# The last image's 3x3 convolution computed by pairs of rows

## The chip, the cores and the metric

The kernel runs on one core of a Trainium2 chip. The metric is the device time of one execution in microseconds (us), as a median of several runs. Engines are named as in the profile: PE is TensorE (matmul), PEld its weight load, DVE is VectorE, ACT is ScalarE, POOL is GpSimd, and SP is SyncE, whose queue issues the transfers (DMA).

## What is computed

The input `x` holds 4 images of 128 channels and 64x64 pixels, all float32. Four layers follow one another, each of the form "x plus a block applied to the group-normalised x": an attention over the 4096 pixels, a 5x5 convolution with built weights, a state-space scan in two directions, and a plain 3x3 convolution. The change touches the last layer alone, and of that only the last image:

```python
def conv2d(x, w, b, stride=1, pad=1):
    y = jax.lax.conv_general_dilated(x, w, window_strides=(stride, stride), padding=[(pad, pad), (pad, pad)], ...)
    return y + b[None, :, None, None]
...
out = conv2d(x, main_w, main_b, stride=1, pad=1)      # 128 channels to 128, 3x3
...
# --- layer 3 (conv_preact) ---
x = x + _L3_conv_ref(_gn(x), ...)
```

(The offset branch of that layer chooses between `out` and `out`, so it isn't computed.)

## The kernel before

Channels lie on the 128 partitions and pixels on the free axis. An image has 4096 pixels, cut into 4 chunks of `CH` = 1024 pixels (16 rows) or 8 pieces of `MM` = 512 (8 rows, one PSUM bank of float32).

The order of the instructions on each engine is written by hand. `scan_core` is the backbone: it emits the ticks of the state-space scan of images 0 to 3 one after the other, and between the half ticks it lets a generator, `images`, emit pieces of all the other work (attention and the 5x5 convolution of later images, the end of earlier ones). A tick puts one product on GpSimd (`drive`, L1027), a decay on ScalarE (L1020), a recurrence on VectorE (L1037), a second product on VectorE or GpSimd (L1040 or L1058), and a sum over states on TensorE (L1072). For images 0 to 2 the last layer (`back`, which calls `conv`) lies beside the scan of later images. For image 3 there is no later image: when the last tick is done, the loop `for _ in chain(end(B - 1, range(PER)), back(B - 1))` emits the rest, and the program ends with it.

The last image's layer in that tail works so. `end` adds the scan's result to the residual `xt` (L1134, L1135, L1137) and collects sums for the group norm. `conv` clears the borders of a padded image `xpm`, calls `group_norm` (a row of small VectorE and GpSimd instructions, ending in `rs_m` L363 and `nb_m` L364), and normalises `xt` into `xpm` on ScalarE in four pieces of 16 rows (L369). Then it runs over the 8 pieces of 512 pixels. For each, 9 products (a 128x128 weight by 128x512 pixels) are summed into one bank `pcm` (L643). A piece's result goes to `finish`, here `put`: one VectorE instruction adds the bank, the bias `MAINB` and the residual `xt` (L1222), and a transfer of 256 KB writes the piece out (L1223).

The 3x3 weights `m3` are the first nine 128x128 matrices of the tile `cw`. That tile holds the 5x5 weights until the last image's 5x5 convolution (`conv_pairs`, L760) is over; a transfer then loads `main_w` over its head, in `front`. `kept` is a copy of those nine matrices of the 5x5 weights in memory, taken at the start for a second pass (`program(True)`), which runs only where a sum of the attention left its range; the test for it (`pfit`, `out_of_range`, L1338 to L1340) are the program's last instructions.

PSUM has eight banks. The tail has one each under the tags `s`, `a`, `z` and `y`, and four in the pool `wide`, in which the scan's decays `da` lie, two tiles of two banks. The pool `hc` holds six tiles of 128x1024 for the scan's products.

Of the kernel before, what the change touches and what calls it, by code (L numbers as in the profile page):

```python
# [24 lines left out]
F32 = mybir.dt.float32  # L25
I32 = mybir.dt.int32
AF = mybir.ActivationFunctionType
ALU = mybir.AluOpType
# [4 lines left out]
P = 128  # L33
GROUPS = 32
GN_EPS = 1e-5
CH = 1024
MM = 512
# [8 lines left out]
PRODUCT, HOP, SLOT, PACE, ENDPACE, AHEAD = 0.86, 1.7, 0.7, 2.8, 1.5, 4  # L46


BQ, BK, BX, BP, CONVB, BD, DSKIP, MAINB, CONVW, ALOG = 0, 1, 2, 3, 4, 5, 6, 7, 8, 12
# [3 lines left out]
def conv_preact_kernel(  # L53
# [16 lines left out]
    nc = tc.nc  # L70
    B, C, H, W = x.shape
    L = H * W
    NCH = L // CH
# [11 lines left out]
    of = out.rearrange("b c h w -> b c (h w)")  # L85
# [3 lines left out]
    dram = ctx.enter_context(tc.tile_pool(name="dram", bufs=2, space=DRAM))  # L89
    ps = ctx.enter_context(tc.tile_pool(name="ps", bufs=1, space=PSUM))  # L90
    pools, ready = {}, set()

    def bank(tag, name):
        return pools.get(tag, ps).tile([P, MM], F32, tag=tag, name=name)
# [32 lines left out]
    def col(i):  # L127
        return vec[:, i : i + 1]
# [93 lines left out]
    cw = const.tile([P, NTAP + 10, C], F32, name="cw")  # L222
    taps5 = cw[:, :NTAP, :]

    m3 = cw[:, : main_w.shape[1], :]
    kept = dram.tile([P, main_w.shape[1], C], F32, tag="kept", bufs=1, name="kept")

    def build_conv_weights(tmp):
        xx_sb = tmp.tile([P, NTAP, C], F32, name="xx_sb")
        nc.sync.dma_start(xx_sb, xhat)  # L230
        id_sb = tmp.tile([P, C], F32, name="id_sb")
        nc.sync.dma_start(id_sb, identity)
        picked = tmp.tile([P, 2, NTAP, C // 2], F32, name="picked")
        for n, (which, table, inds) in enumerate((("xx", wxx, indsxx), ("id", wid, indsid))):
            nr, oc = table.shape[1], table.shape[2]
            acc = picked[:, n]
            one = cw.rearrange("p k c -> p (k c)")[:, : NTAP * oc]
            one = one.rearrange("p (k o) -> p k o", o=oc)
            tab = tmp.tile([P, nr, oc], F32, name=f"tab{which}")
            nc.sync.dma_start(tab, table)  # L240
            ii = tmp.tile([P, NTAP], I32, name=f"ii{which}")
            nc.sync.dma_start(ii, inds.to_broadcast([P, NTAP]))
            fi = tmp.tile([P, NTAP], F32, name=f"fi{which}")
            nc.vector.tensor_copy(fi, ii)

            ng = tmp.tile([P, NTAP], F32, name=f"ng{which}")
            nc.vector.tensor_scalar(ng, fi, 0.0, float(nr), ALU.is_lt, ALU.mult)
            nc.vector.tensor_tensor(fi, fi, ng, ALU.add)
            nc.vector.tensor_scalar(fi, fi, 0.0, float(nr - 1), ALU.max, ALU.min)
            for r in range(nr):  # L250
                hit = tmp.tile([P, NTAP], F32, name=f"hit{which}{r}")
                nc.vector.tensor_scalar(hit, fi, float(r), None, ALU.is_equal)
                hit_b = hit.unsqueeze(2).to_broadcast([P, NTAP, oc])
                tab_b = tab[:, r : r + 1, :].to_broadcast([P, NTAP, oc])
                if r == 0:
                    nc.vector.tensor_tensor(acc, tab_b, hit_b, ALU.mult)
                else:
                    nc.vector.tensor_tensor(one, tab_b, hit_b, ALU.mult)
                    nc.vector.tensor_tensor(acc, acc, one, ALU.add)
                yield HOP  # L260

        for t in range(2):
            def every(ap):
                return ap.rearrange("p k (o t) -> p k o t", t=2)[:, :NTAP, :, t]

            idb = id_sb.rearrange("p (o t) -> p o t", t=2)[:, :, t].unsqueeze(1)
            idb = idb.to_broadcast([P, NTAP, C // 2])
            nc.vector.tensor_tensor(every(xx_sb), every(xx_sb), picked[:, 0], ALU.mult)
            nc.vector.tensor_tensor(every(cw), picked[:, 1], idb, ALU.mult)
            yield HOP  # L270
        nc.vector.tensor_tensor(taps5, taps5, xx_sb, ALU.add)
        for n in range(2):
            row = cw[:, (1 + 2 * n) * 5 :]
            nc.vector.tensor_tensor(
                cw[:, NTAP + n * 5 : NTAP + (n + 1) * 5, :], row[:, :5], row[:, 5:10], ALU.add
            )
        nc.sync.dma_start(kept, m3)

# [1 line left out]
    ASIZE, VSIZE = HP * (W + PAD) + PAD, (H + 2) * (W + 2) + PAD  # L282
# [85 lines left out]
    def normalise(dst, src, gn):  # L368
        nc.scalar.activation(dst, src, AF.Identity, scale=gn[0], bias=gn[1])  # L369
# [244 lines left out]
    def conv(b, xs, tag, st, weights, k, finish, name, residual=False):  # L614

        pad = k // 2
        hp, wp = H + 2 * pad, W + 2 * pad
        size = VSIZE if tag == "V" else ASIZE
        xp = pools["big"].tile([P, size], F32, tag=tag, name=f"xp{name}_{b}")
        xp = xp[:, : hp * wp].rearrange("p (h w) -> p h w", w=wp)  # L620
        nc.gpsimd.memset(xp[:, :pad, :], 0.0)
        nc.gpsimd.memset(xp[:, hp - pad :, :], 0.0)
        nc.gpsimd.memset(xp[:, pad : hp - pad, :pad], 0.0)
        nc.gpsimd.memset(xp[:, pad : hp - pad, wp - pad :], 0.0)
        gn = yield from group_norm(st, f"{name}{b}")
        xh = xs.rearrange("p (h w) -> p h w", w=W)

        def piece(i):
            h0, h1 = i * H // 4, (i + 1) * H // 4
            normalise(xp[:, pad + h0 : pad + h1, pad : pad + W], xh[:, h0:h1, :], gn)  # L630

        piece(0)
        yield HOP / 2
        piece(1)
        done = None
        for i in range(NM):
            if i < 2:
                piece(2 + i)
            acc = bank("saz"[i % 3], f"pc{name}_{b}_{i}")
            for t in range(k * k):  # L640
                dy, dx = divmod(t, k)
                y = i * RPM + dy
                nc.tensor.matmul(  # L643
                    acc.rearrange("p (r w) -> p r w", w=W), weights[:, t, :],
                    xp[:, y : y + RPM, dx : dx + W],
                    start=t == 0, stop=t == k * k - 1 and not residual,
                )
                if t == 2 and done is not None:
                    finish(*done)
                if t % 3 == 2:  # L650
                    yield 3 * PRODUCT
            if residual:
                nc.tensor.matmul(acc, ident, xs[:, bass.ts(i, MM)], start=False, stop=True)
            yield PRODUCT
            done = i, acc
        yield HOP
        finish(*done)

# [483 lines left out]
    def program(safe):  # L1144
        mats4, ynds, ends = {}, {}, {}
        ready.clear()
        if safe:
            nc.sync.dma_start(m3, kept)

        def load(tile, b):  # L1150
            for c in range(NCH):
# [15 lines left out]
        def front(b, xn, v):  # L1167

            xs = large(b + 1, f"xs_{b}")[:, :L]
            st = Sums(f"e{b}")  # L1170
            yield from attention(b, xs, xn, v, st, safe, load(xs, b))
            st2 = Sums(f"s{b}")

            yield from conv_pairs(b, xs, f"A{b % 2}", st, st2, b > 0 or safe)
            if b + 1 == B:
                nc.sync.dma_start(m3, main_w)

            def mat(name):
                return dram.tile([NCH, P, CH], F32, tag=name, name=f"{name}_{b}")

            mats4[b] = (
                [mat("bm"), mat("cm")], mat("dd"), mat("dxd"), mat("xcd"),
                dram.tile([P, L], F32, tag="xsd", bufs=B, name=f"xsd_{b}"),
            )
            ynds[b] = dram.tile([NM, P, MM], F32, tag="ynd", bufs=B, name=f"ynd_{b}")
            operands = yield from scan_prep(b, xs, st2, mats4[b])
            if b + 1 < B:
                return (yield from both(operands, start(b + 1, 10)))
            yield from operands

        def stage(b, pieces, done):

# [19 lines left out]
        def back(b):  # L1212
            xs, st, _ = ends[b]

            def put(i, acc):
                cut = bass.ts(i, MM)
                if b + 1 < B:
                    to = pools["bg"].tile([P, MM], F32, tag="w", bufs=4, name=f"o_{b}_{i}")
                    nc.scalar.activation(to, acc, AF.Identity, bias=col(MAINB))
                else:  # L1220
                    to = xs[:, cut]
                    nc.vector.scalar_tensor_tensor(to, acc, col(MAINB), to, ALU.add, ALU.add)  # L1222
                nc.sync.dma_start(of[b][:, cut], to)  # L1223

            yield from conv(b, xs, "V", st, m3, 3, put, "m", residual=b + 1 < B)

        def both(*gens):

# [173 lines left out]
```

## Time and profile before

| what | value |
|---|---|
| time, median of 3 runs | 4534.42 us (4531.9 to 4534.6) |
| span of the profiled run | 4538.3 us |
| PE busy | 4022.5 us (89%) |
| DVE busy | 3649.1 us (80%) |
| POOL busy | 3636.2 us (80%) |
| ACT busy | 2400.1 us (53%) |
| `pcm` products (L643), all four images | 576 rows, 592 ns in the median |
| `pcm` products of the last image, in the tail | 144 rows, 63.8 us |

How to read it: a product of float32 shows as two rows in the records of PE, so the last image's 72 products are 144 rows. Matmuls are pipelined, so a row's duration is more than its share of the time; the time of a run of products is read from its first start to its last end. "Idle before, releaser" is the time in which an engine had nothing to do, and what ended it. The chain of waits follows back from the last instruction to what each one waited for.

### The profile page before, as it was taken

The page shows a single profiled execution, that of the slowest core. Times are in us where ns is not written, and L with a number is a line of the kernel's source. Part 1 is how long each engine was busy: PE and PEld are TensorE (multiplying, and loading weights), DVE is VectorE, ACT ScalarE, POOL GpSimd, SP SyncE. Part 2 cuts the span into 40 slices and gives each one's busy share as a digit, 9 for nine tenths or more (in the row PEclk, how much of TensorE's full clock was granted, in tenths as well). Part 3 has the DMA queues.
Part 4 walks back from the last instruction along what each step waited for, and adds up shares of the span by engine and source line. Part 5 has one row for each costly group of instructions (what it writes and reads, how often), then busy time and mean ns, then how long its engine had stood idle before and what let it go on. Part 6 is the DMA issues. An engine that isn't in the chain of part 4 may idle for free. (4 is left out here: it accounts for less than half of the span.)

```text
span 4538.3 us, 43660 instructions
## 1 busy us (share of the span) xinstructions
PE 4022.5 (89%) x13568; PEld 1492.3 (33%) x13568; DVE 3649.1 (80%) x3619; ACT 2400.1 (53%) x4420; POOL 3636.2 (80%) x1730
## 2 busy tenths in 40 slices
PE   8999998999999979999999879999999658576767
PEld 4444433333333323333333223333333112121212
DVE  4722106999998978999989879999999699999993
ACT  3333217666665466666654566666654654544441
POOL 3433207999998969999989889999999799999992
PEclk9999999999999989999999989999999878687878
DMA  1000006445544555544545555545445566656561
GB/s 62 6 1 1 5 29 239 175 170 174 175 174 155 181 202 201 175 174 169 179 154 181 185 207 180 169 170 175 175 159 178 211 235 204 231 188 230 186 232 47
DMA packets 210579, 719.48 MB, mean 159 GB/s; under 512 B 24864, under 2 KB 25760, under 8 KB 210208
## 3 DMA queue, kind: packets, MB, share of 16 engines
q1 hardware_dynamic: 208736, 715.87, 44.8%
q8 instruction: 109, 1.79, 0.2%
q14 instruction: 134, 1.10, 0.1%
q10 hardware_dynamic: 1600, 0.73, 0.1%
HBM read 649.07 MB, written 67.44 MB: 158 GB/s over the span
## 5 line engine op out<-in xcount | busy, mean ns | idle before, releaser
L1027 POOL TENSOR_TENSOR db<-dx,br 128x1024 f32<-128x1024 f32 x1024 | 2399.7, 2366 | 234.0 <-DMA dx<-dxd 59.7
L1020 ACT ACTIVATE da<-de,a_neg 128x512 f32<-128x512 f32 (+1 forms) x1795 | 1342.2, 751 | 745.4 <-DVE da L1037 451.2
L464 PE MATMUL sc<-r,x 128*128 128x512 f32 x2048 | 1082.4, 611 | 18.2 <-ACT r L433 12.4
L476 PE MATMUL acc<-pt,v 128*128 128x512 f32 x2048 | 1046.6, 593 | 1.6
L1058 POOL TENSOR_TENSOR hc<-hc,cr 128x1024 f32<-128x1024 f32 x406 | 959.7, 2364 | 14.3 <-ACT last L1053 11.7
L470 ACT ACTIVATE pt<-sc 128x512 f32<-128x512 f32 x1024 | 604.3, 590 | 563.9 <-PE sc L464 555.2
L1072 PE MATMUL y<-hc,sel 128*32 128x512 f32 x4096 | 656.9, 651 | 271.5 <-POOL hc L1058 267.0
L1040 DVE TENSOR_TENSOR hc<-da,cr 128x512 f32<-128x512 f32 (+1 forms) x1067 | 828.4, 776 | 68.9 <-issue 1.8
L1037 DVE TENSOR_TENSOR_SCAN da<-da,last,db 128x512 f32<-128x512 f32 (+1 forms) x464 | 728.2, 1569 | 27.3 <-POOL db L1027 21.7
L1037 DVE TENSOR_TENSOR_SCAN da<-da,da,db 128x512 f32<-128x512 f32 x449 | 577.9, 1287 | 13.6 <-ACT da L1020 12.7
L464 PEld LDWEIGHTS sc<-r,x 128*128 128x128 f32 x2048 | 359.1, 190 | 605.0 <-issue 374.3
L476 PEld LDWEIGHTS acc<-pt,v 128*128 128x128 f32 x2048 | 387.5, 190 | 497.2 <-issue 477.9
L1037 DVE TENSOR_TENSOR_SCAN hc<-da,hc,db 128x512 f32<-128x512 f32 x322 | 413.1, 1283 | 61.2 <-ACT da L1020 30.4
L1037 DVE TENSOR_TENSOR_SCAN hc<-da,last,db 128x512 f32<-128x512 f32 (+1 forms) x304 | 455.9, 1500 | 6.6 <-ACT da L1020 2.4
L518 POOL TENSOR_TENSOR sidep<-sidep,pt 128x512 f32<-128x512 f32 x120 | 170.4, 1420 | 280.0 <-ACT pt L470 277.9
L1072 PEld LDWEIGHTS y<-hc,sel 128*32 128x32 f32 x4096 | 94.7, 111 | 728.5 <-POOL hc L1058 359.5
L643 PE MATMUL pcm<-xpm,cw 128*128 128x512 f32 x576 | 290.5, 652 | 30.5 <-ACT xpm L369 30.5
L760 PE MATMUL pe<-df,cw 128*128 128x512 f32 x640 | 289.5, 598 | 0.0
L518 DVE TENSOR_TENSOR sided<-sided,pt 128x512 f32<-128x512 f32 x120 | 97.2, 810 | 231.0 <-ACT pt L470 229.7
L1037 DVE TENSOR_TENSOR_SCAN da<-da,db 128x512 f32<-128x512 f32 (+1 forms) x154 | 231.2, 1501 | 32.5 <-POOL db L1027 16.4
L498 PE MATMUL zp<-pt,ones 128*32 128x512 f32 x1536 | 204.8, 595 | 5.0 <-DVE xs L562 5.0
L1053 ACT COPY last<-da 128x1 f32<-128x1 f32 x469 | 73.0, 156 | 246.9 <-DVE hc L1040 245.1
(196 smaller groups left out, 2719.5 us busy)
## 6 DMA issues: line engine op xcount, KB each, us to landing
br<-bm SPq DMA_DIRECT2D x512, 512.0 KB, 5.2
cr<-cm SPq DMA_DIRECT2D x512, 512.0 KB, 3.9
de<-dd SPq DMA_DIRECT2D x64, 512.0 KB, 4.6
dx<-dxd SPq DMA_DIRECT2D x64, 512.0 KB, 6.5
x<-in_x_dram SPq DMA_DIRECT2D x16, 512.0 KB, 5.1
xs<-in_x_dram SPq DMA_DIRECT2D x16, 512.0 KB, 5.6
xsd<-xs SPq DMA_DIRECT2D x16, 512.0 KB, 5.1
xcd<-xc SPq DMA_DIRECT2D x16, 512.0 KB, 2.8
```

The lines of the kernel that those rows point to most:

```text
L464: nc.tensor.matmul(sc, xn[:, bass.ts(j, P)], rq[blk], start=True, stop=True)
L470: nc.scalar.activation(pt, sc, AF.Exp)
L476: nc.tensor.matmul(acc[blk], v[:, j, :], ring[:, u % NRING, :], start=j == 0, stop=j == NJT - 1)
L518: eng.tensor_tensor(s, s, ring[:, u % NRING, :], ALU.add)
L643: nc.tensor.matmul(acc.rearrange("p (r w) -> p r w", w=W), weights[:, t, :], xp[:, y : y + RPM, dx : dx + W], start=t == 0, stop=t == k * ...
L760: nc.tensor.matmul(flat(acc), cw[:, w * K5 + dx, :], view(r, dx), start=k == 1, stop=k == total and (n == 0 or not lean),)
L1020: nc.scalar.activation(da, rep["de", b, c, d, g][:, bass.ts(h, size)], AF.Exp, scale=a_neg[:, at(i)])
L1027: nc.gpsimd.tensor_tensor(dbs[i], rep["dx", b, c, d, g], rows["b", b, c, d, q], ALU.mult)
L1037: nc.vector.tensor_tensor_scan(h, da, db[:, cut], before, ALU.mult, ALU.add)
L1040: nc.vector.tensor_tensor(hc[:, cut], h, rows["c", b, c, d, q][:, cut], ALU.mult)
L1058: nc.gpsimd.tensor_tensor(hcs[i], hcs[i], rows["c", b, c, d, q], ALU.mult)
L1072: nc.tensor.matmul(y[r : r + SG, :], sel, hcs[i - KG + 1 + gg][:, bass.ts(h, MM)], start=q == 0, stop=False, tile_position=(0, r), skip_gr ...
```

## The change

Two neighbouring output rows need four input rows. Call these d0 to d3, and the weights of the three rows of a 3x3 kernel g0, g1, g2 (each still with three columns). Then

- e = g0 (d0 - d2), s = (g0 + g1 + g2)/2 (d1 + d2), t = (g0 - g1 + g2)/2 (d2 - d1), o = g2 (d3 - d1)
- upper row = e + s + t, lower row = s - t + o

Four products for each of the three columns give two rows, where the direct way takes six. `conv_last` does this for image 3. Its chunk is 16 output rows, that is 8 pairs, so each of e, s, t, o is a bank of 128x512, and a chunk takes 4 banks and 12 products. It stands in for `conv` in the tail; images 0 to 2 keep `conv`.

- `last_weights` makes the two combined weights (three matrices each, `HSUM` and `HDIF`) by four VectorE instructions over 128x384, emitted when the last image's scan operands are done, early in the last image's scan. They lie in `cw` behind `m3`, so `kept` now saves and restores 15 matrices and not nine.
- `piece(c)` normalises 17, 16, 16 and 15 rows (one ahead of the chunk); the padded image has no columns at the sides, and the products of the outer columns take 63 of the 64 pixels of a row.
- `combine(c)` makes the four sums of rows: d2 - d1 and d3 - d1 on GpSimd, d1 + d2 and d0 - d2 on VectorE, into tiles of the pool `hc`.
- The banks are `s`, `a`, `z`, `y` for the even chunks and the four of `wide` for the odd ones.
- Each chunk ends with a ScalarE copy of t, two GpSimd instructions (add to the upper rows, subtract from the lower ones), two VectorE instructions that add s and the bias, two that add e and o, and one transfer of 512 KB.

The diff's core (the changes of `kept` to 15 matrices, and the unpacking of `put`, are left out):

```diff
+    def last_weights():
+        half, above = cw[:, HSUM : HSUM + 3, :], cw[:, HDIF : HDIF + 3, :]
+        nc.vector.tensor_tensor(half, m3[:, 0:3, :], m3[:, 6:9, :], ALU.add)
+        nc.vector.tensor_scalar(half, half, 0.5, None, ALU.mult)
+        nc.vector.scalar_tensor_tensor(above, m3[:, 3:6, :], -0.5, half, ALU.mult, ALU.add)
+        nc.vector.scalar_tensor_tensor(half, m3[:, 3:6, :], 0.5, half, ALU.mult, ALU.add)
+
+    def conv_last(b, xs, st, finish):
...
+        def combine(c):
+            d = [rows[:, 2 * CK * c + k : 2 * CK * (c + 1) + k - 1 : 2, :] for k in range(4)]
+            made = []
+            for eng, pairs in (
+                (nc.gpsimd, ((2, 1, ALU.subtract), (3, 1, ALU.subtract))),
+                (nc.vector, ((1, 2, ALU.add), (0, 2, ALU.subtract))),
+            ):
+                two = pools["hc"].tile([P, CH], F32, tag="hc", name=f"cb_{b}_{c}_{len(made)}")
+                for n, (i, j, op) in enumerate(pairs):
+                    made.append(flat(two[:, bass.ts(n, MM)]))
+                    eng.tensor_tensor(made[-1], d[i], d[j], op)
+            combined[c] = made
...
+        def products(acc, view, w):
+
+            for n, dx in enumerate((1, 0, 2)):
+                to = slice(max(1 - dx, 0), W - max(dx - 1, 0))
+                of_ = slice(max(dx - 1, 0), W - max(1 - dx, 0))
+                nc.tensor.matmul(
+                    flat(acc)[:, :, to], cw[:, w + dx, :], view[:, :, of_],
+                    start=n == 0, stop=n == 2, skip_group_check=True,
+                )
...
+        piece(0)
+        combine(0)
+        piece(1)
+        combine(1)
+        for c in range(NCH):
+            t_, o_, s_, e_ = banks_of(c)
+            diff, odd, total, even = combined.pop(c)
+            products(t_, diff, HDIF)
+            products(s_, total, HSUM)
+            products(e_, even, 0)
+            products(o_, odd, 6)
+            if c + 2 < NCH:
+                piece(c + 2)
+                combine(c + 2)
+            ts_ = pools["bg"].tile([P, MM], F32, tag="w", bufs=4, name=f"t_{b}_{c}")
+            nc.scalar.copy(ts_, t_)
+            nc.gpsimd.tensor_tensor(part(c, 0), part(c, 0), flat(ts_), ALU.add)
+            nc.gpsimd.tensor_tensor(part(c, 1), part(c, 1), flat(ts_), ALU.subtract)
+            for y, own in enumerate((e_, o_)):
+                nc.vector.scalar_tensor_tensor(
+                    part(c, y), flat(s_), col(MAINB), part(c, y), ALU.add, ALU.add
+                )
+            for y, own in enumerate((e_, o_)):
+                nc.vector.tensor_tensor(part(c, y), flat(own), part(c, y), ALU.add)
+            finish(c)
+            yield HOP
...
-            yield from conv(b, xs, "V", st, m3, 3, put, "m", residual=b + 1 < B)
+            if b + 1 < B:
+                yield from conv(b, xs, "V", st, m3, 3, put, "m", residual=True)
+            else:
+                yield from conv_last(
+                    b, xs, st,
+                    lambda c: nc.sync.dma_start(of[b][:, bass.ts(c, CH)], xs[:, bass.ts(c, CH)]),
+                )
```

More of the change, by code (lines that the diff above doesn't have):

```diff
@@ L225, in conv_preact_kernel @@
     m3 = cw[:, : main_w.shape[1], :]
-    kept = dram.tile([P, main_w.shape[1], C], F32, tag="kept", bufs=1, name="kept")
+    HSUM, HDIF, NKEPT = 9, 12, 15
+    kept = dram.tile([P, NKEPT, C], F32, tag="kept", bufs=1, name="kept")
     def build_conv_weights(tmp):
@@ L276, in build_conv_weights @@
             )
-        nc.sync.dma_start(kept, m3)
+        nc.sync.dma_start(kept, cw[:, :NKEPT, :])
     ASIZE, VSIZE = HP * (W + PAD) + PAD, (H + 2) * (W + 2) + PAD
@@ L657, in conv, with flat, piece, banks_of @@
         finish(*done)
+    def last_weights():
[5 more added lines that the diff above has]
+    def conv_last(b, xs, st, finish):
+        CK = CH // W // 2
+        xp = pools["big"].tile([P, VSIZE], F32, tag="V", name=f"xpl_{b}")
+        rows = xp[:, : (H + 2) * W].rearrange("p (h w) -> p h w", w=W)
+        nc.gpsimd.memset(rows[:, 0, :], 0.0)
+        nc.gpsimd.memset(rows[:, H + 1, :], 0.0)
+        gn = yield from group_norm(st, f"m{b}")
+        xh = xs.rearrange("p (h w) -> p h w", w=W)
+        def flat(t):
+            return t.rearrange("p (h w) -> p h w", w=W)
+        def piece(c):
+            h0, h1 = 2 * CK * c + (c > 0), min(2 * CK * (c + 1) + 1, H)
+            normalise(rows[:, 1 + h0 : 1 + h1, :], xh[:, h0:h1, :], gn)
+        combined = {}
+        def combine(c):
[10 more added lines that the diff above has]
+            combined[c] = made
+        def banks_of(c):
+            if c % 2 == 0:
+                return [bank(tag, f"pl{tag}_{b}_{c}") for tag in "sazy"]
+            two = [
+                pools["wide"].tile([P, CH], F32, tag="da", bufs=2, name=f"pl{n}_{b}_{c}")
+                for n in range(2)
+            ]
+            return [t[:, bass.ts(h, MM)] for t in two for h in range(2)]
+        def products(acc, view, w):
[6 more added lines that the diff above has]
+                )
+        def part(c, y):
+            return xs[:, bass.ts(c, CH)].rearrange("p (h t w) -> p h t w", t=2, w=W)[:, :, y, :]
+        piece(0)
[24 more added lines that the diff above has]
+            yield HOP
@@ L1147, in program @@
         if safe:
-            nc.sync.dma_start(m3, kept)
+            nc.sync.dma_start(cw[:, :NKEPT, :], kept)
         def load(tile, b):
@@ L1189, in front @@
             yield from operands
+            last_weights()
         def stage(b, pieces, done):
@@ L1216, in put @@
                 cut = bass.ts(i, MM)
[L1217 to L1222, printed above, removed]
-                nc.sync.dma_start(of[b][:, cut], to)
-            yield from conv(b, xs, "V", st, m3, 3, put, "m", residual=b + 1 < B)
+                to = pools["bg"].tile([P, MM], F32, tag="w", bufs=4, name=f"o_{b}_{i}")
+                nc.scalar.activation(to, acc, AF.Identity, bias=col(MAINB))
+                nc.sync.dma_start(of[b][:, cut], to)
+            if b + 1 < B:
[5 more added lines that the diff above has]
+                )
         def both(*gens):
```

## The prediction, made before the changed kernel ran

> **What bounds the kernel now.** I read the shares of the page first: PE 89%, DVE and POOL 80% each. They say nothing of this change, since it acts only behind the last scan tick. So I went to the chain of waits, and of it to the last 75 us (columns: start, duration, what).
>
> ```profile
> 4464.01 0.56 POOL rs_m L363
> 4464.64 0.20 POOL nb_m L364
> 4464.86 1.25 ACT xpm L369
> 4466.16 63.86 PE pcm L643 x144
> 4530.04 0.75 DVE xt L1222
> 4530.79 0.07 DVE out_of_range L1339
> ```
>
> From the end of the group norm (`nb_m`, 4464.84) to the end of the last `xt` (4530.79) it is a chain of three pieces, 65.95 us: one normalisation, 72 products without a gap, one addition. Nothing else is on it. The rest of the span (4538.3 - 4530.79 = 7.5 us) is the last transfer and the program's end.
>
> Next, is that stage TensorE at its best? The busy time by stages (columns: stage, its length, PE busy, granted clock, DMA share, GB/s):
>
> ```profile
> 4464.00:4468.00 4.00, 1.84 (x2) 0.50 0.00 0
> 4468.00:4472.00 4.00, 4.00 (x9) 0.78 0.00 0
> 4472.00:4476.00 4.00, 4.00 (x11) 1.00 0.00 0
> 4476.00:4480.00 4.00, 4.00 (x10) 1.00 0.17 66
> ```
>
> The clock is 0.50 when the products begin and 1.00 from about 4470.2 (0.78 over the second stage means half speed for 1.76 of its 4 us). The rest runs at full speed. The VectorE timeline gives the price: `xt` starts at 4476.01 for the first bank and at 4514.59 for the sixth.
>
> ```profile
> 4476.01 0.75 DVE L1222 SCALAR_TENSOR_TENSOR xt<-pcm,vec,xt 128x512 f32<-128x512 f32 x1 [12.09 <-PE pcm L643]
> 4514.59 0.75 DVE L1222 SCALAR_TENSOR_TENSOR xt<-pcm,vec,xt 128x512 f32<-128x512 f32 x1 [6.92 <-PE pcm L643]
> ```
>
> That is 38.58 us for 45 products, 0.857 us each. The first bank took 4476.01 - 4466.16 = 9.85 where 9 x 0.857 = 7.71 would do: the slow clock costs 2.1 us once. VectorE is idle for 6.9 us of each bank, ScalarE and GpSimd all the time. They are what the change uses.
>
> **What the Trainium skill says.** "TensorE: Matmul & The Clock Gate", section "What's actually happening": the array runs at half clock after an idle window of some 3.4 us and is released after about as long of sustained work, whatever the number of products. The trace agrees: 6.9 us idle, then half clock for some 4.0 us. So I keep the 2.1 us as a fixed cost. "GPSIMD Engine Reference", section "1. Specifications": GpSimd shares its interfaces to SBUF with VectorE, with contention where a VectorE instruction reads two SBUF inputs. The trace has a sign of it: the 128x512 additions that the two do beside one another in the first attention (L518) take 1420 and 810 ns, and those of other stages 1271 (L889) and 692 (L1040). I use both as ends below.
>
> **Removed.** 72 products (61.7 us at 0.857 each, plus the 2.1), eight `xt` of 0.75, eight transfers.
>
> **Added on TensorE.** 4 chunks x 4 banks x 3 columns = 48 products. 16 take 512 pixels (0.857), 32 take 8 x 63 = 504 (0.844 in proportion): 13.7 + 27.0 = 40.7, with the clock's 2.1 it is 42.8 us.
>
> **Added ahead of the first product.** Normalising 17 rows where it was 16: 1.25 x 17/16 = 1.33, and 0.04 to the next engine. Then a wait that is new: the first product takes d2 - d1 from GpSimd. The nearest rows are the 5x5 convolution's differences, of the same pattern with every second row:
>
> ```profile
> L684 POOL TENSOR_TENSOR df<-xpe 128x528 f32<-128x528 f32 x12 | 13.3, 1108 | 2.6 <-ACT xpe L369 2.6
> L518 POOL TENSOR_TENSOR sidep<-sidep,pt 128x512 f32<-128x512 f32 x120 | 170.4, 1420 | 280.0 <-ACT pt L470 277.9
> L518 DVE TENSOR_TENSOR sided<-sided,pt 128x512 f32<-128x512 f32 x120 | 97.2, 810 | 231.0 <-ACT pt L470 229.7
> L775 POOL TENSOR_TENSOR xs<-xs,q 128x512 f32<-128x512 f32 x8 | 10.0, 1266 | 98.6 <-ACT q L773 98.6
> L736 DVE SCALAR_TENSOR_TENSOR xs<-pe,xs 128x512 f32<-128x512 f32 x32 | 21.7, 679 | 140.9 <-PE pe L760 137.5 <-PE pe L781 3.4
> ```
>
> 1108 for 528 columns is 1.08 for 512. VectorE does d1 + d2 at the same time, so the upper end is 1.42. I take 1.15 and 0.05 for the hand-over. Behind it on GpSimd are d3 - d1 and the sums of chunk 1, in front of it nothing (the border memsets, each about 0.22, are done during the group norm). VectorE's d1 + d2 (0.69 to 0.81) is ready before the three products of t are over (2.6 us at full clock).
>
> **Beside TensorE, hidden.** A chunk keeps TensorE for 12 x 0.85 = 10.2 us. GpSimd has two sums and two additions: 2 x 1.08 + 2 x 1.27 = 4.7, at most 4 x 1.42 = 5.7. VectorE has two sums (0.69 to 0.81), two of the form of L1222 (0.75) and two additions from PSUM (0.69): 4.3 to 4.5. ScalarE has one piece (1.25) and a copy of t (0.58, as L773). Each is under 10.2, and the sums run two chunks ahead: `combine(c + 2)` is emitted ahead of chunk c's additions, so it doesn't queue behind a wait for chunk c's banks. `combine(3)` on VectorE does: it waits behind o of chunk 0, which comes when chunk 0's products end, and has all of chunks 1 and 2 (some 20 us) for it. On GpSimd the four sums of chunks 0 and 1 take 4 x 1.08 = 4.3 from the first normalisation, while chunk 1 is needed some 11 us later. Eight banks for two chunks: chunk c + 2 needs those of chunk c, free one chunk earlier. I cost all this at nothing; TensorE's products hide it.
>
> **At the end.** In chunk 3, t is ready 7.6 us before the last product ends; copy, GpSimd's pair and VectorE's pair take 0.58 + 2.54 + 1.5 = 4.6 and e another 0.69, so when o's bank is complete only one addition is left: 0.69 + 0.03. The last transfer is 512 KB and not 256. The page has 2.0 us to landing for `xt`'s 256 KB and 2.6 to 2.9 for 512 KB writes (`dd`, `dxd`). Whether the end waits for it (the test value and the last instruction fetches run beside it) the trace doesn't show: 0 to 0.8, I take 0.5.
>
> **Early, in the scan.** `last_weights`: four VectorE instructions of 384 columns, between 0.28 (L190, 128 columns) and 0.69 (512): about 0.55 each, 2.2 us. VectorE is busy 95% or more in the last scan, so 2.2 is the upper bound. But the order of the changed kernel puts them right after the first ticks of image 3, and there the timeline shows:
>
> ```profile
> 3623.75 1.28 DVE L1037 TENSOR_TENSOR_SCAN hc<-da,hc,db 128x512 f32<-128x512 f32 x1
> 3630.33 2.30 DVE L1037 TENSOR_TENSOR_SCAN da<-da,db 128x1024 f32<-128x1024 f32 x1 [5.30 <-POOL db L1027]
> ```
>
> VectorE waits 5.30 us for GpSimd two instructions later, and GpSimd (busy with L894 until 3628) doesn't need the delayed scan before 3635. I cost it at 0. The larger copy `kept` is a transfer in the first attention, and no product waits for it.
>
> **Sum.** New chain: 1.33 + 0.04 + 1.15 + 0.05 + 42.8 + 0.03 + 0.69 = 46.1, against 65.95: 19.9 less. Plus 0.5 for the transfer: 19.4 less, 4534.4 - 19.4 = 4515.0 us. The forecast: faster by 0.43%.
>
> **Rivals.**
> - The sums become part of the path: TensorE waits at each chunk for its first sum. For it: GpSimd is the slowest of the helpers. Against it: 5.7 us of 10.2 even at the worst. If 2.2 to 2.8 us showed at three more chunks, it would be 7 to 8 us: 4522.
> - TensorE's clock doesn't stay at 1.00. For it: in the last scan the mean is 0.72 to 0.93, and every short gap between chunks could bring it back. Against it: the old stage held 1.00 for 60 us. At 0.78 the 40.7 us become 52.2, 11.5 more: 4526.5, which counts as no change.
> - Slower: a wait that I take for harmless (a bank, an `hc` tile, the residual's rows written by two engines) makes the chunks serial. Then each takes 1.3 + 2.2 + 10.2 + 0.6 + 2.5 + 2.9 = 19.7, four 78.8, and with the clock's half speed coming back after each gap 2.1 each: 87 against 66, so 4555. Against it: in the order of the changed kernel the products of chunk 1 wait only for their own sums.
>
> **How the numbers follow.** 0.86 for the forecast, 0.07 for the sums on the path, 0.04 for the clock, 0.03 for serial chunks. The first two are faster: 0.93; the third the same, 0.04; the last slower, 0.03. The range: the bounds of the unknown costs give 1.15 less 0.07 and 0.5 less 0.5 on one side, and on the other 0.27 of GpSimd, 0.3 of the transfer and 2.2 of `last_weights`: 4514.4 to 4517.8. The median of before moves by some 2.7 us between runs, so 4511 below; above I take in the sums on the path: 4522.
>
> **What would show it.** The chain should end with some 96 rows of products lasting 42 to 44 us without an idle stretch over 0.5 us, preceded by one GpSimd difference of 1.1 to 1.4 us, and followed by one addition of 0.7. VectorE's wait at about 3625 us should shrink by some 2 us, and the last scan should end as before, at about 4450. I am wrong if TensorE idles between chunks with GpSimd as the releaser, if the granted clock is below 1.00 after the first 5 us, if a product of 504 columns costs more than one of 512, or if the last scan ends later.

## The result, and the profile after

The changed kernel takes 4523.52 us in the median of 14 runs (4518.83 to 4526.0), the kernel before 4534.45 us beside it (14 runs, 4529.49 to 4536.89): a ratio of 0.9976, 95% interval 0.9968 to 0.9984. It is faster by 10.9 us (0.24%), where 19.4 were forecast, and lies above the forecast range. Direction and bound were right; almost half of the gain is missing. The profiled run spans 4519.0 us.

The chain of waits of the changed kernel, its last 52 us (start, duration, what), answers to the first lines of the prediction:

```profile
4461.28 0.19 POOL nb_m L366
4462.87 1.78 POOL cb L703
4464.70 4.99 PE pls L720 x6
4469.69 2.55 PE plz L720 x6
4472.24 2.55 PE ply L720 x6
4474.79 2.55 PE pla L720 x6
4477.33 10.21 PE pl L720 x24
4487.56 0.59 ACT t L743
...
4509.83 1.27 POOL xt L745
4511.13 0.75 DVE xt L747
4511.88 0.61 DVE xt L751
```

Read it from the top. The group norm ends at 4461.47. The GpSimd difference is there as forecast, but takes 1.78 us and not 1.15. A bank's six rows take 2.55 us as forecast (0.857 + 2 x 0.844 = 2.55). Then, where products without a gap should stand up to the end, the chain leaves TensorE at 4487.6 for a ScalarE copy of t, and at the end it runs over GpSimd and VectorE. (In the part left out it goes from GpSimd's additions of chunks 1 and 2 straight to those of chunk 3, over 15.3 us without a releaser; what those waited for is in the timeline below.) From the group norm's end to the end of the last addition (4513.08) it is 51.6 us: 14.3 less than the 65.95 of before, 5.5 more than the 46.1 of the prediction.

TensorE isn't at fault. The busy time by stages (stage, length, PE busy, clock, DMA share, GB/s):

```profile
4464.00:4468.00 4.00, 3.30 (x4) 0.50 0.00 0
4468.00:4472.00 4.00, 4.00 (x9) 0.86 0.00 0
4472.00:4508.00 36.00, 36.00 (x87) 1.00 0.11 44
```

It starts at 4464.70, has no gap and full clock within 5 us, and is through with its products at 4507.92: 43.2 us, where 42.8 were worked out. The loss is behind it. The timeline of the last 6 us (start, duration, engine, line, operation, idle time before and what ended it), with the end of the products ahead of it:

```profile
4505.63 2.28 PE L720 MATMUL pl<-cb,cw 128*128 128x512 f32 x5
4507.95 0.58 ACT L743 COPY t<-pl 128x512 f32<-128x512 f32 x1 [17.25 <-PE pl L720]
4508.61 1.26 POOL L744 TENSOR_TENSOR xt<-xt,t 128x512 f32<-128x512 f32 x1 [15.34 <-ACT t L743]
4509.83 1.26 POOL L745 TENSOR_TENSOR xt<-xt,t 128x512 f32<-128x512 f32 x1
4509.91 0.75 DVE L747 SCALAR_TENSOR_TENSOR xt<-pl,vec,xt 128x512 f32<-128x512 f32 x1 [1.68 <-POOL xt L744]
4511.13 0.75 DVE L747 SCALAR_TENSOR_TENSOR xt<-pl,vec,xt 128x512 f32<-128x512 f32 x1 [0.47 <-POOL xt L745]
4511.80 1.28 DVE L751 TENSOR_TENSOR xt<-pl,xt 128x512 f32<-128x512 f32 x2
```

The copy of t in chunk 3 waits 17.25 us for TensorE and starts 0.03 us after the *last* product (4505.63 + 2.28 = 4507.91), though t's own three products were over 7.6 us earlier. So the whole chain of copy, two GpSimd and four VectorE instructions stands behind TensorE: 5.2 us. (Ends of products are the profile's modelled ends. The next product starts 0.17 us ahead of such an end; where an expectation below says that a copy follows its products by 0.2 us, it counts from there.)

The second loss lies 900 us earlier. The VectorE timeline around `last_weights` (L669 to L672), and the GpSimd instructions beside it:

```profile
3617.56 0.69 DVE L1136 TENSOR_TENSOR hc<-da,cr 128x512 f32<-128x512 f32 x1
3618.17 1.17 DVE L669 TENSOR_TENSOR cw<-cw 128x384 f32<-128x384 f32 x1
3619.36 2.44 DVE L670 TENSOR_SCALAR cw<-cw 128x384 f32<-128x384 f32 x1
3621.83 2.64 DVE L671 SCALAR_TENSOR_TENSOR cw<-cw 128x384 f32<-128x384 f32 x1
3624.51 2.58 DVE L672 SCALAR_TENSOR_TENSOR cw<-cw 128x384 f32<-128x384 f32 x1
3627.01 1.21 DVE L1133 TENSOR_TENSOR_SCAN hc<-da,db 128x512 f32<-128x512 f32 x1
3628.33 1.28 DVE L1133 TENSOR_TENSOR_SCAN hc<-da,hc,db 128x512 f32<-128x512 f32 x1
3630.94 2.30 DVE L1133 TENSOR_TENSOR_SCAN da<-da,db 128x1024 f32<-128x1024 f32 x1 [1.33 <-ACT da L1116]
```

```profile
3616.56 2.35 POOL L1154 TENSOR_TENSOR hc<-hc,cr 128x1024 f32<-128x1024 f32 x1
3618.86 5.20 POOL L990 TENSOR_TENSOR xc<-delta,xc 128x1024 f32<-128x1024 f32 x2
3624.00 5.29 POOL L1123 TENSOR_TENSOR db<-dx,br 128x1024 f32<-128x1024 f32 x2
```

The four take 8.8 us where 2.2 were forecast, the last three about as long each as a GpSimd product beside them. VectorE's idle time of 5.30 us behind them should have shrunk by some 2 us. It is gone altogether, since it wasn't long enough, and in its place stands a new wait of 1.33 for a decay.

### The profile page after: what moved, and what is told of

Read it like the earlier page. It is cut to its first block, busy times and chain, and to the rows that moved or that the text cites. A ratio compares the mean times of both kernels' runs of the same rounds, so it can differ in the third digit from the quotient of the medians.

```text
span 4519.0 us, 43613 instructions
## 1 busy us (share of the span) xinstructions
PE 3998.1 (88%) x13520; PEld 1482.2 (33%) x13520; DVE 3672.3 (81%) x3639; ACT 2401.3 (53%) x4424; POOL 3658.3 (81%) x1744
## 5 line engine op out<-in xcount | busy, mean ns | idle before, releaser
L466 PE MATMUL sc<-r,x 128*128 128x512 f32 x2048 | 1080.8, 610 | 18.1 <-ACT r L435 12.4
L1154 POOL TENSOR_TENSOR hc<-hc,cr 128x1024 f32<-128x1024 f32 x406 | 959.2, 2363 | 16.9 <-ACT last L1149 14.3
L1136 DVE TENSOR_TENSOR hc<-da,cr 128x512 f32<-128x512 f32 (+1 forms) x1067 | 828.4, 776 | 68.5 <-issue 1.3
L1133 DVE TENSOR_TENSOR_SCAN da<-da,last,db 128x512 f32<-128x512 f32 (+1 forms) x464 | 728.1, 1569 | 21.9 <-POOL db L1123 16.5
L1133 DVE TENSOR_TENSOR_SCAN da<-da,da,db 128x512 f32<-128x512 f32 x449 | 577.8, 1287 | 14.3 <-ACT da L1116 13.5
L645 PE MATMUL pcm<-xpm,cw 128*128 128x512 f32 x432 | 228.7, 672 | 23.6 <-ACT xpm L371 23.6
```

The lines of the kernel that those rows point to most:

```text
L466: nc.tensor.matmul(sc, xn[:, bass.ts(j, P)], rq[blk], start=True, stop=True)
L645: nc.tensor.matmul(acc.rearrange("p (r w) -> p r w", w=W), weights[:, t, :], xp[:, y : y + RPM, dx : dx + W], start=t == 0, stop=t == k * ...
L1133: nc.vector.tensor_tensor_scan(h, da, db[:, cut], before, ALU.mult, ALU.add)
L1136: nc.vector.tensor_tensor(hc[:, cut], h, rows["c", b, c, d, q][:, cut], ALU.mult)
L1154: nc.gpsimd.tensor_tensor(hcs[i], hcs[i], rows["c", b, c, d, q], ALU.mult)
```

## The experiments

Theory A, formed from these traces: (1) the copy of t waits for the last writer of the whole double-bank tile in which t shares room with o (the products run in the order t, s, e, o; in the odd chunks t and o are the halves of one tile, s and e of the other); (2) VectorE and GpSimd take turns where both work from SBUF, which stretches `last_weights` beside the scan's GpSimd products, and the first sums of the tail. Each expectation below was written before its run. A median of 5 runs moves by some us, so the sizes are read from the traces, and the times only say which way. All "below" and "above" are against the kernel before, run beside it.

**Weights at the end.** `last_weights()` leaves `front`:

```diff
             yield from operands
-            last_weights()
...
+            last_weights()
             for _ in chain(end(B - 1, range(PER)), back(B - 1)):
```

> The four instructions of last_weights move from the first ticks of the last image's scan to the tail, behind the last scan tick, where VectorE and GpSimd wait 10 us for the group norm. Theory A (in the scan each of the four waits for a GpSimd instruction to end, since both have two inputs in SBUF; 8.8 us in the trace of the changed kernel where 2.2 were forecast, of which only 5.3 fell into VectorE's idle time): with GpSimd idle the four take 2.0 to 2.3 us in all, the rest of the tail is as in the changed kernel, and the time falls by 3 to 5 us, to some 4519 to 4520. Rival B (8.8 us is what these instructions take by themselves): 8 to 9 us at the end too, still hidden by the group norm. Rival C (the scan absorbs them): the time stays at 4523.5.

4513.67 us, 18.1 below (ratio 0.9958, 0.9945 to 0.9972). The VectorE timeline of this run:

```profile
4447.04 0.55 DVE L669 TENSOR_TENSOR cw<-cw 128x384 f32<-128x384 f32 x1
4447.63 0.36 DVE L670 TENSOR_SCALAR cw<-cw 128x384 f32<-128x384 f32 x1
4448.02 0.56 DVE L671 SCALAR_TENSOR_TENSOR cw<-cw 128x384 f32<-128x384 f32 x1
4448.61 0.56 DVE L672 SCALAR_TENSOR_TENSOR cw<-cw 128x384 f32<-128x384 f32 x1
```

The same four instructions, with GpSimd idle (its next instruction, at 4459.32, comes after 13.17 us of idle time): 2.0 us in all, about what the prediction had. Rival B falls: they are not long by themselves. The tail is as it was, 51.2 us from the group norm's end to the last addition. The time fell by more than the 3 to 5 us expected, within what five runs can tell.

**Last chunk in single banks.**

```diff
-            if c % 2 == 0:
+            if c % 2 == 1:
                 return [bank(tag, f"pl{tag}_{b}_{c}") for tag in "sazy"]
```

> Even chunks take the two double-bank tiles, odd chunks (the last one among them) the four single banks; nothing else changes. Theory A (the copy of t waits for the whole double-bank tile, in which o is written last): in chunk 3 the copy follows t's three products by 0.2 us, its GpSimd pair and the s additions lie beside the products of s, e and o, the stretch from the last product to the last addition falls from 5.5 us to 0.7, and the time falls by 4.5 to 5 us, to 4518.5 to 4519. In chunks 0 and 2 the copy waits for o instead, at no cost. Rival (the end waits for the last transfer or the test value anyway): the stretch shortens but the time stays within 1 us of 4523.5.

4514.26 us, 17.5 below (0.9961, 0.9948 to 0.9975). In this run's ScalarE timeline the copy of chunk 3 is at

```profile
4501.32 0.59 ACT L743 COPY t<-pls 128x512 f32<-128x512 f32 x1 [1.96 <-PE pls L720]
```

right behind t's products, 7.6 us ahead of the end of the last one, and on VectorE one addition is left:

```profile
4508.97 0.69 DVE L751 TENSOR_TENSOR xt<-pla,xt 128x512 f32<-128x512 f32 x1 [1.86 <-PE pla L720]
```

The last product ends at 4508.94 and this addition at 4509.66: 0.7 us, as the prediction had it, where the changed kernel has 5.2 (4507.92 to 4513.08). In the changed kernel the test value was ready 4.8 us before the last addition; here the test is behind that addition again, and the program's end is 6.9 us after it where it was 5.9. So the stretch is 4.4 us shorter, TensorE's slow start cost 0.5 less in this trace, the program's end takes 1.0 more, and the span behind the group norm falls by 3.9 (57.5 to 53.6). The time fell by more than the 4.5 to 5 us expected, again within what five runs can tell.

**The direct convolution with the weights.** The kernel before, with `last_weights` (not used) and the larger `kept` (the unpacking of `put`, left out here, is taken back too):

```diff
-            if b + 1 < B:
-                yield from conv(b, xs, "V", st, m3, 3, put, "m", residual=True)
-            else:
-                yield from conv_last(...)
+            yield from conv(b, xs, "V", st, m3, 3, put, "m", residual=b + 1 < B)
```

> The direct convolution of the kernel before, with last_weights still run early in the scan (its results are not used) and the larger saved copy. Theory A (last_weights costs the scan time): 3 to 5 us above the kernel before, 4537.5 to 4539.5, and the four instructions take 8 to 9 us as in the changed kernel. Rival C (absorbed): 4534.5 within 1 us.

4538.09 us (13 runs), 6.4 above (1.0013, 1.0005 to 1.0022). Rival C falls: without the new convolution too the kernel is slower, by more than the 3 to 5 us expected, but with these in the interval (2 to 10 us). The four instructions take 8.7 us here too (1.04, 2.44, 2.65, 2.58). No run has the larger copy by itself. It isn't the cause as far as the traces show: the comparison of twelve traces further below starts behind it, and the kernels with the weights at the end carry it as well.

**Both moves.**

> The weights at the end and the last chunk in single banks together. Theory A: the two gains add, 8 to 10 us below the changed kernel, 4513.5 to 4515.5, which is what was forecast for the changed kernel. Rival C for the weights: 4518.5 to 4519, no better than the last chunk's move alone.

4511.5 us, 20.2 below (0.9951, 0.9938 to 0.9965). That is the forecast of 19.4 less, within its interval, and 9.3 us more than the changed kernel's gain. The single moves' medians would add to more (7.2 and 6.6); their sum isn't to be trusted beyond the intervals. In the trace it is 46.7 us from the group norm's end to the last addition.

**Sum first.** On the kernel with both moves:

```diff
-            products(t_, diff, HDIF)
-            products(s_, total, HSUM)
+            first = [(t_, diff, HDIF), (s_, total, HSUM)]
+            for acc, view, w in first[::-1] if c == 0 else first:
+                products(acc, view, w)
```

> As the kernel with both moves, and in chunk 0 the products of s go ahead of those of t: TensorE begins with a sum of VectorE and not with a difference of GpSimd. Theory A (VectorE and GpSimd take turns, one two-input instruction in SBUF at a time; VectorE's first sum takes 0.68 us, GpSimd's first difference starts behind it and is over at 1.77): the first product starts 0.75 us after the normalisation and not 1.82, and the chain shortens by 1.0 to 1.1 us. Rival (the two only slow one another, sharing alike): the sum too takes 1.5 or more, and the gain is under 0.3 us.

4511.68 us, 20.8 below (0.9957, 0.9943 to 0.9971). The chain of this run:

```profile
4454.55 1.30 ACT xpl L371
4455.87 0.70 DVE cb L703
4456.62 12.71 PE pl L720 x24
```

VectorE's sum takes 0.70, and the first product starts 2.1 us after the group norm's end, against 3.2 with both moves alone. Turns, as expected, and the sharing rival falls. But the first 24 rows take 12.71 us and not 12.14 as there, so of the 1.1 us only 0.6 is left up to the last addition: the slow clock at the start costs now 2.5, now 1.9 us. The times (4511.68 and 4511.5) can't tell the two kernels apart.

**All sums on VectorE.** On the kernel with both moves:

```diff
-                (nc.gpsimd, ((2, 1, ALU.subtract), (3, 1, ALU.subtract))),
+                (nc.vector, ((2, 1, ALU.subtract), (3, 1, ALU.subtract))),
```

> As the kernel with both moves, and all four sums of each chunk are made on VectorE, t's first; GpSimd keeps the additions of t only. Theory A (turns): each of the sixteen sums takes 0.68 us where those of the changed kernel took 1.7 in the median, the first product starts 0.75 us after the normalisation, 1.0 to 1.1 earlier, and since GpSimd's work was in turns anyway nothing gets longer: the sums of chunks 0 to 2 end no later than before. Rival (each engine needs its time, and together they are faster): the twelve early sums take longer in all than the 10.1 us in which both engines made them.

4512.05 us, 20.5 below (0.9956, 0.9941 to 0.9970). The sums' line in the changed kernel (count, minimum, median and maximum in ns, first and last start), and then in this run:

```profile
L703 DVE TENSOR_TENSOR cb<-xpl x8: 682/1748/1757, 4462.8 to 4478.6; 128x512 f32<-128x512 f32 x8
L703 POOL TENSOR_TENSOR cb<-xpl x8: 1262/1708/1771, 4462.9 to 4476.7; 128x512 f32<-128x512 f32 x8
```

```profile
L703 DVE TENSOR_TENSOR cb<-xpl x16: 678/684/1200, 4456.4 to 4477.2; 128x512 f32<-128x512 f32 x16
```

The twelve early sums are over in 7.3 us here (4456.41 to 4463.73), and took 10.1 when two engines made them: 1.2 us for two sums on VectorE alone, 1.7 for one on each engine. The rival falls. The second engine brought nothing but waiting. From the group norm's end to the last addition it is 46.0 us, the 46.1 of the prediction.

**The changed kernel again.**

> The changed kernel itself beside the others on the same chip, for the sizes: theory A has it 8 to 10 us above the kernel with both moves (some 3.9 from the last chunk's wait, net of a shorter end of the program, and 3 to 6 from the weights in the scan), and 9 to 11 below the kernel before.

4521.35 us (9 runs), 11.2 below (0.9976, 0.9965 to 0.9986), and 9.3 to 10.8 above the three kernels with both moves and more that ran beside it (sum first, all sums on VectorE, test early). That is about what was expected. In this trace the weights in the scan cost more than in the others. Their first instruction waited through three GpSimd products:

```profile
3615.57 6.57 DVE L669 TENSOR_TENSOR cw<-cw 128x384 f32<-128x384 f32 x1
```

```profile
3614.68 4.75 POOL L990 TENSOR_TENSOR xc<-delta,xc 128x1024 f32<-128x1024 f32 x2
3619.36 2.37 POOL L1123 TENSOR_TENSOR db<-dx,br 128x1024 f32<-128x1024 f32 x1
```

So the engine that waits doesn't always get the next turn.

**Test early.** On the kernel with the sum first, the test (`fit` to `out_of_range`) is put in a function that runs between `end` and `back`:

```diff
-            for _ in chain(end(B - 1, range(PER)), back(B - 1)):
-                pass
+            for _ in end(B - 1, range(PER)):
+                pass
+            if not safe:
+                range_test()
+            for _ in back(B - 1):
+                pass
```

> As the kernel with the sum first, and the test for the second pass is made beside the last group norm and not behind the last addition. In the changed kernel, where the test value came 4.8 us ahead of the last addition, the program ended 5.9 us after that addition; with both moves the test follows it and the end is 7.0 after it. Theory A (the end waits for the test value as the later of the two): the program ends 5.9 us after the last addition, 1.0 us less, so with the sum first 2.0 to 2.1 us below the kernel with both moves. Rival (the end waits for the last transfer): within 0.2 us of the kernel with the sum first alone.

4510.6 us, 21.9 below (0.9950, 0.9936 to 0.9964). In the traces the program ends 5.9 us after the last addition (4502.81 to 4508.7), where it ends 7.0 after with the sum first alone: the test value was the later of two things by 1.1 us. The time is 1.1 us below that of the sum first alone, less than five runs can tell. What the remaining 5.9 us wait for, the last transfer or the program's own close, no run here tells.

**t beside s.** The changed kernel, with another pairing in the double-bank tiles (t with s, o with e):

```diff
-            return [t[:, bass.ts(h, MM)] for t in two for h in range(2)]
+            return [t[:, bass.ts(h, MM)] for h in range(2) for t in two]
```

> The changed kernel with another pairing in the double-bank tiles of the odd chunks: t with s, o with e (there it was t with o, s with e). The last chunk stays in double-bank tiles. Theory A (a reader waits for the last writer of its tile, not of its bank): the copy of t in chunk 3 starts 0.2 us after the products of s, 2.55 us after those of t and 5.1 us ahead of the last product; e's addition waits for o; from the last product to the end of the last addition 1.4 us, where the changed kernel has 5.5. Rival (a double-bank tile holds its readers back until the chunk is over, whatever the pairing, or the delay is not the tile's): the stretch stays at 5.5.

4517.69 us (6 runs), 13.9 below (0.9969, 0.9957 to 0.9981). ScalarE and VectorE at the end of this run:

```profile
4503.24 0.59 ACT L743 COPY t<-pl 128x512 f32<-128x512 f32 x1 [12.15 <-PE pl L720]
```

```profile
4508.33 1.29 DVE L751 TENSOR_TENSOR xt<-pl,xt 128x512 f32<-128x512 f32 x2 [1.15 <-PE pl L720]
```

The last product ends at 4508.31, and the last addition 1.3 us later, where 1.4 were expected. The copy starts 5.1 us ahead of the end of the products, when s is complete and not t, and both last additions wait for o, though e was complete 2.55 us earlier. So it is the tile whose last writer counts, and the double banks as such are harmless.

**All moves.** Weights at the end, single banks last, all sums on VectorE, test early.

> Weights at the end, last chunk in single banks, all sums on VectorE, test value early. Theory A: from the group norm's end to the last addition 45.9 to 46.1 us, as forecast for the changed kernel, the end of the program 5.9 behind it, the scan free of the weights: 20 to 23 us below the kernel before. Rival: no better than the kernel with the two moves, 18 to 20 below.

4509.7 us, 21.9 below (0.9950, 0.9937 to 0.9964). The group norm's end to the last addition is 46.8 us here and not the 45.9 to 46.1 expected, since the slow clock cost 3.2 us in this trace (13.40 us for the first 24 rows). It beats both kernels, and so do the kernel with both moves and the three that build on it; among these five the medians (4509.7 to 4512.05) can't be told apart.

## Why the prediction was wrong

Right, point by point: the bound (TensorE, once, behind the scan), the price of a product (2.55 us for three of a bank) and the 42.8 us for all 48 (43.2 measured); no gap between chunks, full clock after the start; the helpers hidden during chunks 0 to 2.

**"At the end" failed first.** "In chunk 3, t is ready 7.6 us before the last product ends" is true, but I took the copy to follow it. In the changed kernel t shares a tile of two banks with o, and t's reader waits for o. Instead of one addition (0.72 us) copy, GpSimd's pair and VectorE's four stand behind TensorE: 5.2 us. The runs with single banks and with t beside s show it, one by taking the wait away, the other by moving it to s. The kernel's text showed the pairing, and the order of its instructions showed the copy waiting for TensorE; which product it waited for I didn't ask. Chunk 1, of the same tiles, has the same wait, hidden under chunk 2, so I would have found it only by asking for the last chunk.

**"Early, in the scan" failed second.** "About 0.55 each, 2.2 us" was the price on an idle machine (2.0 measured there). Beside the scan's GpSimd products it was 8.8, and I had put what the scan loses by it at nothing. I had the warning in hand, GpSimd's shared interface, and used it for the sums of the tail alone. It was in the trace of before as well. There the first instructions of a group norm meet GpSimd's products (VectorE timeline):

```profile
3714.30 0.17 DVE L320 TENSOR_REDUCE gn_sums<-su_m 128x2 f32<-128x16 f32 x1
3714.50 2.53 DVE L321 TENSOR_SCALAR gcols<-gn_sums 128x2 f32<-128x2 f32 x1
3717.06 0.16 DVE L322 TENSOR_TENSOR aw_m<-gcols,aw_m 128x1 f32<-128x1 f32 x1
```

Two elements per partition in 2.53 us, in other places 0.17: L321 ends 0.5 us after the GpSimd product that ran beside it (4.69 us for two, from 3711.87). L320, a reduction, took its usual 0.17 beside the same product. A longest time far above the minimum, in a group of tiny instructions, is a reason to look for such a wait.

How much it cost: VectorE's next scan came 9.0 us later relative to GpSimd's work (the four with the gaps between them). 5.30 of it fell into the idle time, and 1.33 came as a new wait for ScalarE's decay: 9.0 - 5.3 + 1.3 = 5.0. Measured in the traces, from the start of GpSimd's four additions to `delta` to the first 1024-wide scan: 21.5 to 21.6 us in four of the five traces with the weights in the scan (24.4 in the fifth, the changed kernel again), and 16.5 to 16.6 in all seven without them. The rest of the scan gives a part back. From the same start to that of the last GpSimd product of the scan the five take 835.1 to 838.9 us, mean 836.7, the seven 831.2 to 834.8, mean 833.1: 3.7 us net.

The sign that I had named, a last scan that ends later than at about 4450, doesn't show this: the start of those four additions alone lies between 3605.2 and 3613.8 us in the twelve traces, and the trace of before, at 3613.8, is of a run 5.7 us above the median. That GpSimd is what stretched the weights rests on the move to where it is idle and on the traces; the one run that changes GpSimd's work alone beside VectorE is that of the sums.

**A smaller term.** GpSimd's first difference took 1.77 (upper end in the prediction 1.42), since VectorE's sum went ahead of it: 0.6 us, 0.7 with the small gaps around it. (The 0.69 us of L1040, which I took for VectorE's lower end, is of an instruction with one input in PSUM, so it said nothing about two engines in SBUF; the sums do take 0.68 alone.)

**The sum.** 5.5 for the tail (4.4 at its end, 0.7 at its start, 0.4 of clock and products), 3.7 for the weights, and 2.1 back because the program's end came 5.9 us after the last addition, where I had 7.5 + 0.5. (The 0.5 for a larger last transfer doesn't show in any trace: with both moves the end takes 7.0 us.) So 19.4 - 7.1 = 12.3 us; measured 10.9, with an interval of some 7 to 15. My rival "serial chunks" had the right kind of cause, a wait taken for harmless, but it was priced for all chunks and given 0.03; that it could strike the last chunk alone, where nothing hides it, I didn't consider.

## What to carry to other kernels

For the last piece of a kernel ask of each reader not only whether its data is ready but what else has to be written before its wait is over: give values that are read early a tile of their own, or let the last piece use one. Price a VectorE instruction with two inputs in SBUF, or a `tensor_scalar` there, by what GpSimd runs beside it, and if it is off the path, put it where GpSimd is idle. Before sharing small sums between these two engines, try one alone.

## What the runs showed of the hardware

- VectorE and GpSimd take turns, by whole instructions, in the forms seen here. In the run with the sum first VectorE's sum of 128x512 kept its 0.70 us, while GpSimd's, begun 0.04 us later, took 1.78; a VectorE instruction of two elements took 2.53 us beside a GpSimd product of 2.37. Sums of 128x512 take 0.68 us on VectorE with GpSimd idle and 1.26 on GpSimd beside VectorE instructions that read PSUM (chunk 3 of the changed kernel), and 1.75 (VectorE) and 1.71 (GpSimd) side by side; VectorE instructions of 384 columns take 0.36 to 0.56 alone and mostly 2.42 to 2.65 beside GpSimd products of 2.36, once 6.57. A pair of sums, at 1.7 us, is 0.2 shorter than the two added up, so the records overlap a little. The Trainium skill's "GPSIMD Engine Reference", section "1. Specifications", names the contention, for VectorE instructions "in a 2-port perf mode or with two SBUF inputs". The traces agree and give the size. L670 has one SBUF input and waited like the others; by "VectorE: DVE Perf Modes", section "The perf-mode tier table (the rule you actually need)", such an instruction on float32 in SBUF runs at twice the rate, and here it takes 0.36 us alone where L669, of two inputs, takes 0.55, so both fit. The scan's products with one input in PSUM weren't stretched: L1136 took 0.69 us for 512 columns at 3617.56, beside GpSimd's L1154.
- TensorE's slow start isn't the fixed 2.1 us that the prediction had. After the same 6.9 us of idle time it cost 2.1 us in the kernel before and 3.2 in the direct convolution with the weights; in the changed kernels, after 7.5 to 8.8 us, 1.9 to 3.2 (first 24 rows 12.1 to 13.4 us, 10.2 at full clock). A gain of 1 us ahead of the first product can vanish in it.
